# Cross attention: outputs turned in 32x32 blocks, operations dealt out over the steps, second round in front of the first, hand-over in source order

## The chip, the cores and the metric

The kernel runs on one core of a Trainium2 chip. The metric is the time of one execution on the device in microseconds (us), taken as the median of several runs. Engines are named as the profile names them: PE (TensorE, matrix multiply) and PEld (its weight loads), DVE (VectorE), ACT (ScalarE), POOL (GpSimd), SP (SyncE, which here only issues DMAs).

## The reference

One pre-norm decoder layer on x of 32 x 128 x 512 in float32: self attention, cross attention, then a mixture of experts with a shared expert.

```python
x = x + _L0_attn_ref(_layernorm(x, axis=-1), ...)             # differential attention, 16 heads, causal
x = x + _L0_xattn_ref(_layernorm(x, axis=-1), ctx_2048, ...)   # this change
x = x + _L0_ffn_ref(_layernorm(x, axis=-1), ...)               # 32 experts, 6 per token, and a shared expert

# cross attention: 128 channels of 512 positions; 8 heads of 16 channels; for each of 32 batches
q, k, v = split_heads(Wq x + bq), split_heads(Wk c + bk), split_heads(Wv c + bv)
q, k = rotary(q), rotary(k)
p = softmax(q k^T / 4)                      # 512 x 512 for each head
out = Wo (p v) + bo

# experts: scores = sigmoid(x @ gate_w); of 4 groups of 8 experts the two with the best maxima are masked out,
# the best 6 of the rest are taken, weights divided by their sum;
# expert(x) = (silu(x @ w_gate) * (x @ w_up)) @ w_down; the shared expert has the same form for all tokens
```

## The kernel before, in words

**Stages.** Self attention runs to about 870 us and writes x1 to DRAM. The cross attention (class `CrossAttention`) follows to about 2058 us. Behind it lie two groups of the shared expert (class `Shared`, 4 batches of 128 tokens a group), among which the rest of the routing is put (the hand-over). From about 2212 us the routed experts run (class `Experts`, 208 tiles of 128 token slots), from about 3748 us the other six groups of the shared expert.

**A step of the cross attention.** Work is cut into 512 steps (b, side, c, pair): 32 batches, two sides (even and odd heads), four chunks of 128 positions, two pairs of heads. In a first round `maxima` (two matmuls of 32 rows by 512 columns, L621) computes scores and DVE takes row maxima from PSUM (L625). When the 8 steps of a side are done, `turn_maxima` transposes the maxima and adds them to the queries (L633). Eleven steps later the second round, `exponentials`, computes the same scores the other way round, already shifted (L644), and ACT takes exp (L648). `weigh` multiplies values and exponentials (L659), in two halves before and behind the two rounds of a step, once for each 8 steps. A column of ones beside the values gives the denominators. The two rounds of one step use different row quarters of the array.

**The other operations of a batch.** `plan` gives each a step number: `sooner` ones come in front of the two rounds of a step, `later` ones behind them. In order: `load`, `project` and `rotate` for keys and queries (DVE shuffle L590, five POOL operations), `measure` and `normalize`; after weighing, ACT copies the weighed outputs out of PSUM (`xu`, L665), `divide` turns them with 8 TensorE transposes (L674), takes reciprocals (L677) and multiplies (L680), `turn_out` turns them back with 4 transposes (L83) and an ACT copy, `leave` applies Wo (L697) and adds (L701). Then `measure_out`, `normalize_out`, `hand_over` (h3 and its transpose to DRAM), `router`, and the routing: `groups`, `choose`, `take` (L928, L933), `count` (two matmuls L940, L941), `slots_of`, six times `enter` (one indirect DMA from POOL, L957). A batch's routing ends some 60 steps after its attention, so the operations of four batches lie among the steps of a fifth.

**What sets the order.** `CrossAttention.run` holds PE, DVE, ACT and POOL to source order (`manual_schedule`). An instruction that waits holds all behind it on its engine. Everything else, the hand-over among it, is ordered by a scheduler of the framework. PSUM is used through 4 buffers of two banks each (`Common.banks`); an operation that takes one waits until the last reader of its former content is done.

**Hand-over before.** Group 0 of the shared expert runs with `between` called 8 times; each of six calls runs 16 steps' worth of the remaining operations (`cross.rest(16)`), then come `routing.tiles` (which expert has which tiles) and a DMA. Then `Experts.__init__` gathers the tables from DRAM (L1215), turns them (L1224, L1234) and works out addresses (L1239 to L1257); `begin` starts tokens and weights; group 1 runs; then the expert loop.

Of the kernel before, what the change touches and what calls it, by code (L numbers as in the profile page):

```python
# [10 lines left out]
F32 = mybir.dt.float32  # L11
# [7 lines left out]
P = 128  # L19
# [444 lines left out]
class CrossAttention:  # L464
# [12 lines left out]

    NH, C = 8, 16
# [172 lines left out]
    def weigh(self, b, side, half):  # L651
# [11 lines left out]
        if half:  # L663
            self.out[b, side] = self.p2.tile([P, E], F32, name="xu")
            self.nc.scalar.copy(self.out[b, side], po.pop((b, side)))  # L665

    def divide(self, b):

        nc, TC, Q, C, out = self.nc, self.TC, self.Q, self.C, self.out
        tr = self.cm.banks()  # L670
        for side in range(2):
            u = out.pop((b, side))
            for c in range(TC):
                nc.tensor.transpose(tr[:, side, ts(c, P)], u[:, ts(c, P)], self.cm.ident)  # L674
        tr = tr.rearrange("p s (x r) -> p s x r", r=2 * C)
        rs = self.p2.tile([P, 2, TC * Q], F32, name="xrs")
        nc.vector.reciprocal(rs, tr[:, :, :, C])  # L677
        out[b] = self.p2.tile([P, TC * Q, 2, C], F32, name="xo")
        for side in range(2):
            nc.vector.tensor_tensor(  # L680
                out[b][:, :, side, :], tr[:, side, :, 0:C],
                rs[:, side].unsqueeze(2).broadcast_to([P, TC * Q, C]), ALU.mult,
            )

    def turn_out(self, b):
        tr = self.cm.turn4(self.out.pop(b).rearrange("p x s c -> p (x s c)"))
        self.out[b] = self.p2.tile([P, self.TC, P], F32, name="xoT")
        self.nc.scalar.copy(self.out[b], tr)
# [5 lines left out]
    def leave(self, b):  # L694
# [3 lines left out]
            py, self.wT["o"], self.out.pop(b).rearrange("p t x -> p (t x)"), start=True, stop=True  # L698
# [30 lines left out]
    def plan(self, load_shared):  # L729

        S, later, sooner, routing = self.S, self.later, self.sooner, self.routing
        for b in range(self.B):
# [16 lines left out]
            sooner.put(at + 29, self.measure_out, b)  # L749
            later.put(at + 31, self.normalize_out, b)  # L750
            later.put(at + 38, self.hand_over, b)
            later.put(at + 40, self.router, b)
            later.put(at + 45, routing.groups, b)
            sooner.put(at + 53, routing.choose, b)
            later.put(at + 53, routing.take, b)
            later.put(at + 55, routing.count, b)
            sooner.put(at + 61, routing.slots_of, b)
            for k in range(TOPK):
                later.put(at + 63 + 5 * k // 2, routing.enter, b, k)
        later.put(20, load_shared)  # L760
        for b in range(self.B):
            sooner.put(2 * S * b - 11, self.measure, b)
# [12 lines left out]
    def advance(self, count, end=None):  # L775
# [3 lines left out]
        for _ in range(count):  # L779
# [6 lines left out]
            self.sooner.run(n)  # L786
            if 0 <= n < len(steps):
                self.maxima(*steps[n])
            if 0 <= n - behind < len(steps):
                self.exponentials(*steps[n - behind])  # L790
# [27 lines left out]
class Routing:  # L818
# [61 lines left out]
    def groups(self, b):  # L880

        nc = self.nc
        s = self.score.pop(b)
# [5 lines left out]
        )  # L889
        top = self.small("g_top", [P, 8])  # L890
# [202 lines left out]
class Shared:  # L1093
# [6 lines left out]
    def __init__(self, cm, pool, w, h3T_d, sum_d, out):  # L1100
        self.cm, self.pool, self.w, self.h3T_d, self.sum_d, self.out = cm, pool, w, h3T_d, sum_d, out
        self.NB = h3T_d.shape[0]
        self.hTs = {}

    def load(self, g):
        G = self.G
        if g * G < self.NB and g not in self.hTs:
            self.hTs[g] = self.pool.tile([P, G, EC, P], F32, name="s_hT", bufs=2)
            self.cm.nc.sync.dma_start(
                out=self.hTs[g], in_=self.h3T_d[ts(g, G)].rearrange("b p c t -> p b c t")  # L1110
            )

    def group(self, g, final, between=lambda: None):
# [4 lines left out]
        self.load(g)  # L1118
        self.load(g + 1)
        hT = self.hTs.pop(g)  # L1120
        gu = pool.tile([P, n + 1, G, P], F32, name="s_gu")
        for m in range(n):
            pgu = cm.banks().rearrange("p two (i t) -> p two i t", i=G)
            for i, part in enumerate((w.gate, w.up)):
                for c in range(EC):
# [3 lines left out]
                    )  # L1129
            act = pool.tile([P, G, P], F32, name="s_act", bufs=2)  # L1130
# [43 lines left out]
class Experts:  # L1174
# [210 lines left out]
    def begin(self, first, end):  # L1385

        self.first, self.end, self.last = first, end, None
        for i in range(first, first + 3):
            self.tokens(i)
# [187 lines left out]
```

## Time and profile before

| what | value |
|---|---|
| median of 3 runs | 4100.53 us (4096.46 to 4104.73) |
| profiled execution | 4099.66 us, span of its instructions 4098.0 us |
| mean granted TensorE clock | 0.992 |
| DMA | 386 MB moved by the core's queues, mean 94 GB/s |
| cross-attention loop, per batch | 37.13 us |
| hand-over, last weighing to first expert matmul | 153.7 us |
| one group of the shared expert | 57.5 us |

The page of a profile gives the busy time of each engine, the busy share in 40 slices of the span (a digit is tenths), the chain of work that ended last, and groups of equal instructions. A group's row reads: line, engine, operation, output <- inputs, shapes, count, busy us and mean ns of one. Views of the trace give a timeline (start, duration, engine, line, operation; in brackets the idle time in front and what ended it), waits (who waited for whom), windows (busy us of each engine in a stretch) and single lines (minimum, median and maximum in ns). A matmul of 512 columns in float32 has two records. Records of one engine overlap a little, so the distance from start to start is shorter than a duration.

### The profile page before, as it was taken

What the parts mean: (1) busy time and instruction counts of PE and PEld (TensorE: products, weight loads), DVE (VectorE), ACT (ScalarE), POOL (GpSimd) and SP (SyncE); (2) the same over time, 40 slices, a digit from 0 to 9 for tenths busy, and PEclk for the clock granted to TensorE, in tenths of its full rate; (3) what the DMA queues carried; (4) which work ended last, traced back from release to release, by engine and by line L of the source; (5) the groups of instructions that cost most, each with busy time, mean ns of one, the idle gap of its engine ahead of it and who ended that gap; (6) DMA issues with size and microseconds to landing.
All of it is one profiled execution on the core that took longest, in us unless ns stands there. A gap on an engine that the chain in (4) does not pass through costs nothing. (4 is left out here: it accounts for less than half of the span.)

```text
span 4098.0 us, 59001 instructions
## 1 busy us (share of the span) xinstructions
PE 3979.2 (97%) x20404; PEld 2081.9 (51%) x20404; DVE 2192.4 (54%) x3461; ACT 1245.6 (30%) x1791; POOL 2241.5 (55%) x2420
## 2 busy tenths in 40 slices
PE   7999999989999999999979999999999999999999
PEld 5666666533344444434335555555555555554444
DVE  5777777777888888888722333333333333332111
ACT  3333333235555555555510111111111111111000
POOL 3444444443555555555444777777777777772000
PEclk9999999999999999999999999999999999999999
DMA  3111110021111111111134777686777776774110
GB/s 105 32 32 31 32 32 27 32 80 38 46 45 40 45 45 45 42 42 45 32 125 117 173 171 195 139 198 155 175 158 174 167 182 155 179 179 115 52 62 31
DMA packets 282785, 386.24 MB, mean 94 GB/s; under 512 B 147792, under 2 KB 175056, under 8 KB 282448
## 3 DMA queue, kind: packets, MB, share of 16 engines
q0 software_dynamic: 62912, 109.85, 15.0%
q1 hardware_dynamic: 77680, 186.52, 14.0%
q10 hardware_dynamic: 141888, 86.01, 7.6%
q8 instruction: 165, 2.70, 0.3%
q14 instruction: 140, 1.15, 0.1%
HBM read 616.47 MB, written 142.02 MB: 185 GB/s over the span
## 5 line engine op out<-in xcount | busy, mean ns | idle before, releaser
L1310 POOL DMA_INDIRECT e_xr<-h_d,e_run_of x832 | 849.4, 1021 | 296.3 <-issue 246.8
L625 DVE TENSOR_REDUCE nm<-ps 128x2 f32<-128x1024 f32 x512 | 623.2, 1224 | 199.6 <-PE ps L621 131.4
L648 ACT ACTIVATE xp<-ps 128x1024 f32<-128x1024 f32 x512 | 516.8, 1023 | 432.0 <-PE ps L644 430.3
L1340 DVE TENSOR_TENSOR e_gu<-e_act,ps 128x352 f32<-128x352 f32 x208 | 108.4, 521 | 956.4 <-ACT e_act L1339 956.4
L1371 PE MATMUL ps<-wd,e_guT 128*128 128x512 f32 (+1 forms) x1248 | 571.7, 594 | 2.2 <-issue 2.1
L621 PE MATMUL ps<-xk,xq 32*128 32x512 f32 x2048 | 564.3, 635 | 6.7 <-DVE xres L403 4.3
L644 PE MATMUL ps<-xqn,xk 32*128 32x512 f32 x2048 | 548.1, 638 | 0.6 <-DVE xqn L633 0.6
L1335 PE MATMUL ps<-wg,e_xT 128*128 128x352 f32 x1664 | 527.7, 459 | 4.2 <-DMA wg<-in_L_ffn_w_gate_dram 3.4
L1335 PE MATMUL ps<-wu,e_xT 128*128 128x352 f32 x1664 | 527.1, 460 | 2.0 <-DMA wu<-in_L_ffn_w_up_dram 1.9
L1335 PEld LDWEIGHTS ps<-wg,e_xT 128*128 128x128 f32 x1664 | 314.8, 189 | 238.3 <-issue 103.4
L1335 PEld LDWEIGHTS ps<-wu,e_xT 128*128 128x128 f32 x1664 | 316.4, 190 | 179.7 <-DMA wu<-in_L_ffn_w_up_dram 3.7
L1376 POOL DMA_INDIRECT sum_d<-e_y,e_into x208 | 338.3, 1627 | 116.7 <-issue 65.0
L1339 ACT ACTIVATE e_act<-ps 128x352 f32<-128x352 f32 x208 | 96.3, 463 | 892.8 <-PE ps L1335 818.4
L1371 PEld LDWEIGHTS ps<-wd,e_guT 128*128 128x128 f32 (+1 forms) x1248 | 238.0, 191 | 247.5 <-issue 204.1
L1375 ACT ACTIVATE e_y<-ps,e_weight 128x512 f32<-128x512 f32 x208 | 142.9, 687 | 421.6 <-PE ps L1371 407.2
L621 PEld LDWEIGHTS ps<-xk,xq 32*128 32x128 f32 x2048 | 158.6, 183 | 220.6 <-ACT xp L648 100.4
L957 POOL DMA_INDIRECT table_d<-entry,at x192 | 196.6, 1024 | 108.7 <-DMA table_d<-entry,at 55.0
L1361 DVE STREAM_TRANSPOSE e_guT<-e_gr 96x384 f32<-96x384 f32 (+1 forms) x416 | 230.3, 554 | 37.9 <-DMA e_gr<-e_gu_d 30.6
L659 PE MATMUL ps<-xp,v 128*32 128x512 f32 x2048 | 247.1, 598 | 3.0 <-ACT xp L648 2.6
L1322 DVE STREAM_TRANSPOSE e_xT<-e_xr 128x512 f32<-128x512 f32 x208 | 226.7, 1090 | 6.4 <-DMA e_xr<-h_d,e_run_of 6.4
L239 POOL TENSOR_SCALAR k<-kz,a_keep,a_extra 128x256 f32<-128x256 f32 x128 | 69.8, 555 | 252.4 <-ACT kz L238 252.4
L644 PEld LDWEIGHTS ps<-xqn,xk 32*128 32x128 f32 x2048 | 152.8, 183 | 37.6 <-DVE nm L625 25.6
(265 smaller groups left out, 5071.9 us busy)
## 6 DMA issues: line engine op xcount, KB each, us to landing
wg<-in_L_ffn_w_gate_dram SPq DMA_DIRECT2D x208, 704.0 KB
wu<-in_L_ffn_w_up_dram SPq DMA_DIRECT2D x208, 704.0 KB
wd<-in_L_ffn_w_down_dram SPq DMA_DIRECT2D x208, 576.0 KB
e_gu_d<-e_gu ACTq DMA_DIRECT2D x208, 192.0 KB
e_gr<-e_gu_d ACTq DMA_DIRECT2D x208, 192.0 KB
wd<-in_L_ffn_w_down_dram SPq DMA_DIRECT2D x208, 128.0 KB
e_xr<-h_d,e_run_of POOLq DMA_INDIRECT x832
xin<-in_x_dram SPq DMA_DIRECT2D x32, 256.0 KB
```

What stands on the lines that cost most here:

```text
L621: self.nc.tensor.matmul(sc[:, i, :], q[rows, ts(c, P)], k[rows, :], start=True, stop=True)
L625: self.nc.vector.tensor_reduce(at[:, self.ROW[side], 2 * pair : 2 * pair + 2], sc, AX.X, ALU.max, negate=True)
L644: self.nc.tensor.matmul(sc[:, i, :], k[rows, ts(c, P)], q[rows, :], start=True, stop=True)
L648: self.nc.scalar.activation(e, sc, AF.Exp)
L659: self.nc.tensor.matmul(po[b, side][ts(j, 32), :], self.v2[b % 2][:, c, 2 * j + side, :], es[j // 2][:, j % 2, :], start=c == 0, stop=c == ...
L957: self.nc.gpsimd.indirect_dma_start(out=self.table_ds[k % 2][:, :], out_offset=bass.IndirectOffsetOnAxis(ap=self.at[b][:, k : k + 1], axis=0),
L1310: self.cm.nc.gpsimd.indirect_dma_start(out=xr[:, t, :], out_offset=None, in_=self.h3_d.rearrange("t (q f) -> (t q) f", q=self.Q), in_offse ...
L1322: self.cm.nc.vector.transpose(xT.rearrange("p c (t i) -> p c t i", t=self.Q), self.xr.pop(i).rearrange("p t (j c) -> p c t j", c=EC),)
L1335: nc.tensor.matmul(pgu[:, half, 0:M], t[:, c, :], w[:, c, :], start=c == 0, stop=c == EC - 1)
L1361: self.cm.nc.vector.transpose(t[rows, 0:n, :].rearrange("p c (t i) -> p c t i", t=self.Q), g[rows, :, 0 : 32 * n].rearrange("p t (j c) -> ...
L1371: nc.tensor.matmul(py, t[:n, c, :], self.wd[s][:n, c, :], start=c == 0, stop=c == len(M_CHUNKS) - 1)
L1376: nc.gpsimd.indirect_dma_start(out=self.sum_d[:, :], out_offset=bass.IndirectOffsetOnAxis(ap=self.into[:, i : i + 1], axis=0), in_=y[:, :] ...
```

## The change

Five things are done.

1. *Outputs turned in blocks.* DVE transposes the weighed outputs of a side out of PSUM in blocks of 32 x 32 (two instructions a batch, in `weigh`) into one tile `xu` of both sides. `divide` takes reciprocals and multiplies in one instruction for both sides; `turn_out` is one more DVE block transpose. The 12 TensorE transposes and 3 ACT copies of a batch are gone, and with them two PSUM buffers.
2. *Step numbers.* `measure`, `measure_out`, `normalize_out` come 1 or 2 steps earlier, `groups` is cut in two (`sigmoid` first), the routing operations come 1 or 2 steps later.
3. *Order in a step.* `exponentials` stands in front of `maxima`.
4. *Hand-over.* It is held to source order on PE, DVE, ACT and POOL. Two groups of the shared expert carry 33 calls of `cross.rest(2)`, with `between` also called in the middle of each chunk and in the down projection. A third group, which stood at the end, is moved in front of the experts and carries the tables' work, which is cut in `fetch`, `arrange`, `turn_tables`, `places`, `first_tokens`.
5. *Loads.* The first tokens of the shared expert (`load_tokens`) and the rows that a group adds to (`load_rows`) are loaded earlier; the tiles `s_hT` have a pool of their own.

```diff
         if half:
-            self.out[b, side] = self.p2.tile([P, E], F32, name="xu")
-            self.nc.scalar.copy(self.out[b, side], po.pop((b, side)))
+            if side == 0:
+                self.out[b] = self.p2.tile([P, 2, E // 32, 32], F32, name="xu", bufs=1)
+            self.nc.vector.transpose(
+                self.out[b][:, side].rearrange("p k r -> p (k r)"), po.pop((b, side))
+            )
     def divide(self, b):
-        nc, TC, Q, C, out = self.nc, self.TC, self.Q, self.C, self.out
-        tr = self.cm.banks()
-        for side in range(2):
-            u = out.pop((b, side))
-            for c in range(TC):
-                nc.tensor.transpose(tr[:, side, ts(c, P)], u[:, ts(c, P)], self.cm.ident)
-        tr = tr.rearrange("p s (x r) -> p s x r", r=2 * C)
-        rs = self.p2.tile([P, 2, TC * Q], F32, name="xrs")
-        nc.vector.reciprocal(rs, tr[:, :, :, C])
-        out[b] = self.p2.tile([P, TC * Q, 2, C], F32, name="xo")
-        for side in range(2):
-            nc.vector.tensor_tensor(
-                out[b][:, :, side, :], tr[:, side, :, 0:C],
-                rs[:, side].unsqueeze(2).broadcast_to([P, TC * Q, C]), ALU.mult,
-            )
+        nc, C = self.nc, self.C
+        u, n = self.out.pop(b), E // 32
+        rs = self.p2.tile([P, 2, n], F32, name="xrs")
+        nc.vector.reciprocal(rs, u[:, :, :, C])
+        self.out[b] = self.p2.tile([P, n, 2, C], F32, name="xo")
+        nc.vector.tensor_tensor(
+            self.out[b].rearrange("p k s c -> p s k c"), u[:, :, :, 0:C],
+            rs.unsqueeze(3).broadcast_to([P, 2, n, C]), ALU.mult,
+        )
     def turn_out(self, b):
-        tr = self.cm.turn4(self.out.pop(b).rearrange("p x s c -> p (x s c)"))
-        self.out[b] = self.p2.tile([P, self.TC, P], F32, name="xoT")
-        self.nc.scalar.copy(self.out[b], tr)
+        o = self.out.pop(b)
+        self.out[b] = self.p2.tile([P, E], F32, name="xoT")
+        self.nc.vector.transpose(self.out[b], o.rearrange("p k s c -> p (k s c)"))
...
-            sooner.put(at + 29, self.measure_out, b)
-            later.put(at + 31, self.normalize_out, b)
+            sooner.put(at + 27, self.measure_out, b)
+            later.put(at + 29, self.normalize_out, b)
             later.put(at + 38, self.hand_over, b)
             later.put(at + 40, self.router, b)
-            later.put(at + 45, routing.groups, b)
-            sooner.put(at + 53, routing.choose, b)
-            later.put(at + 53, routing.take, b)
-            later.put(at + 55, routing.count, b)
-            sooner.put(at + 61, routing.slots_of, b)
+            later.put(at + 43, routing.sigmoid, b)
+            later.put(at + 46, routing.groups, b)
+            sooner.put(at + 55, routing.choose, b)
+            later.put(at + 55, routing.take, b)
+            later.put(at + 56, routing.count, b)
+            sooner.put(at + 63, routing.slots_of, b)
             for k in range(TOPK):
-                later.put(at + 63 + 5 * k // 2, routing.enter, b, k)
+                later.put(at + 65 + 5 * k // 2, routing.enter, b, k)
         later.put(20, load_shared)
+        later.put(2 * S * (self.B - 2), load_tokens)
         for b in range(self.B):
-            sooner.put(2 * S * b - 11, self.measure, b)
+            sooner.put(2 * S * b - 12, self.measure, b)
...
             self.sooner.run(n)
+            if 0 <= n - behind < len(steps):
+                self.exponentials(*steps[n - behind])
             if 0 <= n < len(steps):
                 self.maxima(*steps[n])
-            if 0 <= n - behind < len(steps):
-                self.exponentials(*steps[n - behind])
...
+    def load_rows(self, g):
+        if g not in self.x2s:
+            self.x2s[g] = []
+            for pair in range(self.G // 2):
+                x2 = self.pool.tile([P, 2, E], F32, name="s_x2", bufs=2)
+                self.cm.nc.sync.dma_start(out=x2, in_=self.rows_of(g, pair))
+                self.x2s[g].append(x2)
...
+    def fetch(self):
+        nc = self.cm.nc
+        for j in range(self.NT):
+            self.got[j] = [
+                self.p2.tile([P, E], F32, name=("e_y", "e_xT")[j % 2])[:, 0 : 2 * P].rearrange(
+                    "p (s o) -> p s o", o=2
+                )
+                for i in range(len(self.table_ds))
+            ]
+            for t, table_d in zip(self.got[j], self.table_ds):
+                nc.gpsimd.indirect_dma_start(
+                    out=t.rearrange("p s o -> p (s o)"),
+                    out_offset=None,
+                    in_=table_d.rearrange("(n s) o -> n (s o)", s=P),
+                    in_offset=bass.IndirectOffsetOnAxis(ap=self.rows[:, j : j + 1], axis=0),
+                    bounds_check=table_d.shape[0] // P - 1,
+                )
+        nc.gpsimd.memset(self.gu_s, 0.0)
+        nc.gpsimd.iota(self.row_i, pattern=[[0, 2]], base=self.T + 1, channel_multiplier=1)
+    def arrange(self, j):
+        nc = self.cm.nc
+        got = self.got[j]
+        nc.vector.tensor_tensor(got[0], got[0], got[1], ALU.add)
+        runs = self.spread[j] = self.p2.tile([P, self.Q, self.Q, 32], F32, name="e_xr", bufs=3)
+        slots = got[0][:, :, 0].rearrange("p (b t a) -> p t a b", b=self.Q, t=self.Q)
+        for t in range(self.Q):
+            nc.vector.tensor_copy(
+                runs[:, t].rearrange("p q (a b) -> p q a b", b=self.Q),
+                slots[:, t].unsqueeze(1).broadcast_to([P, self.Q, 32 // self.Q, self.Q]),
+            )
+    def turn_tables(self):
+        nc, cm = self.cm.nc, self.cm
+        self.entry_ps = cm.banks().rearrange("p o (j t) -> p o j t", j=EC)
+        self.parts_ps = cm.banks().rearrange("p o (t j x) -> p (o t) j x", t=2, j=2)
+        for j in range(self.NT):
+            got, runs = self.got.pop(j), self.spread.pop(j)
+            for o in range(2):
+                nc.tensor.transpose(self.entry_ps[:, o, j, :], got[0][:, :, o], cm.ident)
+            for t in range(self.Q):
+                nc.tensor.transpose(
+                    self.parts_ps[:, t, j, :], runs[:, t].rearrange("p q i -> p (q i)"), cm.ident
+                )
+    def places(self):
+        nc, cp, T, n_tiles = self.cm.nc, self.cp, self.T, self.n_tiles
+        entry = self.entry_ps.rearrange("p o j t -> p o (j t)")[:, :, 0:n_tiles]
+        self.weight = cp.tile([P, n_tiles], F32, name="e_weight")
+        nc.vector.tensor_copy(self.weight, entry[:, 1, :])
+        row_i, row = self.row_i, self.row
+        nc.vector.tensor_scalar(row_i[:, 1:2], row_i[:, 1:2], -T - 1, None, ALU.add)
+        nc.vector.tensor_scalar(row_i[:, 1:2], row_i[:, 1:2], 5, None, ALU.logical_shift_right)
+        nc.vector.tensor_copy(row, row_i)
+        self.run_of = cp.tile([P, self.Q, self.NT * P], I32, name="e_run_of")
+        nc.vector.tensor_scalar(
+            self.run_of, self.parts_ps.rearrange("p t j x -> p t (j x)"), float(self.Q),
+            float(-self.Q), ALU.mult, ALU.add,
+        )
+        nc.vector.tensor_scalar(self.run_of, self.run_of, 0.0, row[:, 1:2], ALU.max, ALU.add)
+        none = cp.tile([P, n_tiles], F32, name="e_none")
+        nc.vector.tensor_scalar(none, entry[:, 0, :], 0.0, row[:, 0:1], ALU.is_equal, ALU.mult)
+        self.into = cp.tile([P, n_tiles], I32, name="e_into")
+        nc.vector.scalar_tensor_tensor(self.into, entry[:, 0, :], -1.0, none, ALU.add, ALU.add)
+    def first_tokens(self):
+        for i in range(self.first, self.first + 3):
+            self.tokens(i)
...
-        todo = [lambda: cross.rest(16)] * 6 + [
+        shared.use(s_pool, s_w)
+        en = mybir.EngineType
+        in_order = {en.PE, en.DVE, en.Activation, en.Pool}
+        todo = [lambda: cross.rest(2)] * 33 + [
             lambda: routing.tiles(eid, fresh, rows, used, usual),
             lambda: nc.sync.dma_start(out=sum_d[T : T + P, :], in_=rest),
         ]
-        EARLY = 2
-        shared.group(0, False, between)
+        EARLY = 3
+        with tc.manual_schedule(engines=in_order):
+            for g in range(EARLY - 1):
+                shared.group(g, False, between)
+            while todo:
+                between()
+    e_ctx = ctx.enter_context(ExitStack())
+    with tc.manual_schedule(engines=in_order):
+        experts = Experts(
+            cm, e_ctx, table_ds, h3_d, sum_d, w_gate, w_up, w_down, eid, fresh, rows, n_tiles
+        )
+        shared.load_rows(EARLY - 1)
+        experts.begin(0, usual)
+        experts.fetch()
+        nothing = lambda: None
+        todo += [nothing] * 3 + [
+            lambda: experts.arrange(0),
+            lambda: experts.arrange(1),
+            nothing,
+            experts.turn_tables,
+            experts.places,
+            experts.first_tokens,
+        ]
+        shared.group(EARLY - 1, False, between)
         while todo:
             between()
-    experts = Experts(
-        cm, e_ctx, table_ds, h3_d, sum_d, w_gate, w_up, w_down, eid, fresh, rows, n_tiles
-    )
-    experts.begin(0, usual)
-    for g in range(1, EARLY):
-        shared.group(g, False)
     experts.run()
```

## The prediction

> **What bounds the kernel now.** I read the page first: which engine is busy, then in which slices it isn't.
>
> ```profile
> span 4098.0 us, 59001 instructions
> PE 3979.2 (97%) x20404; PEld 2081.9 (51%) x20404; DVE 2192.4 (54%) x3461; ACT 1245.6 (30%) x1791; POOL 2241.5 (55%) x2420
> PE   7999999989999999999979999999999999999999
> ```
>
> TensorE is busy for 97% of the span, so time is saved by taking work off it or by closing its gaps. The change touches two stretches: the cross-attention loop (about 905 to 2058 us) and the hand-over behind it (slice 21 of 40). The table of windows gives one batch of the loop, then the hand-over from the last weighing matmul to the first expert matmul, then one undisturbed group of the shared expert.
>
> ```profile
> 1414.79:1451.92 37.13, 36.51 (x243) 15.02 (x242) 30.01 (x51) 21.87 (x27) 21.05 (x30) 1.00 0.14 44
> 2058.20:2211.94 153.74, 131.41 (x352) 62.28 (x351) 34.36 (x103) 17.40 (x26) 54.88 (x74) 0.93 0.40 127
> 3747.96:3805.50 57.54, 57.54 (x145) 26.35 (x145) 5.49 (x8) 3.74 (x7) 1.55 (x1) 1.00 0.31 97
> ```
>
> Columns: length, busy us of PE, PEld, DVE, ACT, POOL, granted clock, DMA share, GB/s. A batch takes 37.13 us with DVE busy for 30.0. But a busy PE also counts a matmul that runs alone where two could run side by side. That is read from the timeline of TensorE:
>
> ```profile
> 1421.22 1.13 PE L621 MATMUL ps<-xk,xq 32*128 32x512 f32 x4
> 1422.02 1.13 PE L644 MATMUL ps<-xqn,xk 32*128 32x512 f32 x4
> 1423.08 0.41 PE L940 MATMUL ps<-taken,before 128*128 128x32 f32 x2
> 1440.87 1.09 PE L674 MATMUL ps<-ident,xu 128*128 128x128 f32 x8
> 1443.29 0.63 PE L83 MATMUL ps<-ident,xo 128*128 128x128 f32 x4 [0.20 <-DVE xo L680]
> 1450.87 1.12 PE L580 MATMUL ps<-cx,kT 128*128 128x512 f32 x2 [0.41 <-DVE nm L625]
> ```
>
> The first-round (L621) and second-round (L644) matmuls of a step start together and take 1.07 us from start to next start. Here L644 comes 0.80 late and the step takes 1.86. Summing start distances: 16 steps x 1.07 = 17.1; weighing 4 x 1.85 = 7.4; three projections 1.05 each; values 1.09; two turns of maxima and h3, 0.59 each; count 0.56; router 1.01; the transposes of xu 1.02 and xo 0.55. That is 33.7. The other 3.45 of the 37.13 are late partners and waits.
>
> The hand-over's waits, from the timeline:
>
> ```profile
> 2062.50 5.53 PE L1126 MATMUL ps<-s_hT,sg 128*128 128x512 f32 x8 [4.23 <-DMA s_hT<-h3T_d]
> 2088.47 0.41 PE L940 MATMUL ps<-taken,before 128*128 128x32 f32 x2 [2.80 <-DVE taken L933]
> 2101.99 0.38 PE L940 MATMUL ps<-taken,before 128*128 128x32 f32 x2 [3.34 <-DVE taken L933]
> 2130.54 7.38 PE L1158 MATMUL ps<-sd,s_gu 128*128 128x512 f32 x12 [7.25 <-DVE s_gu L1132]
> 2154.66 0.54 PE L1224 MATMUL ps<-ident,e_y 128*128 128x128 f32 x2 [2.40 <-DVE e_y L1222]
> ```
>
> With three smaller ones (1.33, 0.68, 0.31) they add to 22.3. Two groups at 57.5 and 9.5 of small matmuls need 124.5 of the 153.7, so 29.2 is lost; the 7 beyond the waits are matmuls at a lower clock (0.93 here; the 5.53 above against 3.60 later).
>
> **The change, part by part: the loop.** TensorE loses 12 transposes per batch: 1.02 + 0.55, so its work is 32.1. ACT loses three copies (two of 0.585, one of 0.580). DVE gains two transposes of a 128x512 out of PSUM: no row has it; by L339 (128x768, 974 ns) scaled, 0.67; by L386 (698, from SBUF), 0.70; I take 0.67, about 0.60 from start to next start. It gains one transpose out of SBUF (L386: 0.70, interval 0.65). The two products of 0.42 become one of 128x512 with both inputs in SBUF.
>
> ```profile
> L352 DVE TENSOR_TENSOR o<-u,rs x64: 668/693/1528, 75.4 to 859.9; 128x512 f32<-128x512 f32 x64
> L928 DVE TENSOR_TENSOR hits<-number,picked x32: 346/1334/1368, 1010.4 to 2101.0; 128x192 f32<-128x192 f32 x32
> ```
>
> [...] If it always met a 1.28 us product of the rotation, the row's maximum (1.53) applies, 0.83 more. L928 shows the same spread: 1.33 in the loop, where it starts behind a rotation product on POOL, 0.35 in the hand-over. In the new order `take` comes two steps later, after POOL's rotation of the keys, and POOL's rotation of the queries ends some 3 us before the product. So I take 0.69 for the product and 0.35 for `hits`, and keep the other ends. DVE is then about 30.5 per batch: no bound by itself.
>
> Then the order. In the program as built, the PSUM buffer of a step's maxima is mostly that of the exponentials one step before, and buffers of exponentials wait for reductions. Times from the rows: an ACT exp starts 1.28 after its matmuls, lasts 1.02, and frees the buffer 0.05 later (2.35 in all); a reduction starts 1.17 after its matmuls, the next DVE work 1.14 later, the buffer is free 1.28 after its start (1420.74 to 1422.02 for the late L644 above). I follow one batch from the first weighing half at step 5 (modulo 16), t = 0. Weighing, step, weighing: step 6 at 4.77. Step 7's maxima wait for step 6's exp: 7.12, 0.69 lost. Its reduction at 8.29, `take` from 9.43 (0.40 + 0.54): `count`, which TensorE reaches at 9.26, starts at 10.37, 1.11 lost. Queued behind it on TensorE are the router and all of step 9, and DVE waits for both. Count and router 1.57: step 9 at 11.94, step 10's maxima at 14.29 (0.69 lost), its reduction at 15.46, the moved measure_out 1.08, step 11's reduction at 17.68, the next weighing at 18.96 (0.41 lost). 4.77 later step 14, step 15's maxima at 26.08 (0.19 lost), reduction at 27.25. From there DVE doesn't pause: reduction 1.14, divide 1.05, 1.14, turn_out 0.65, 1.14, turned maxima 0.62, 1.14, then leave's sum frees a buffer 0.80 later: step 4's maxima at 34.93 (1.86 lost on the way), with the projection the next batch starts at 37.05. Losses 4.97 + work 32.1 = 37.05. So the 1.57 saved is given back, mostly to the wait of `count` and the DVE run behind `divide`: 37.05 against 37.13. Bounds: losses as now, 33.7 + 3.45 - 1.57 - 0.2 = 35.4; [...] 37.05 + 0.98 + 0.83 = 38.9. Over 31 batches: -2.5 (from -54 to +55). The drain after the last maxima has the transposes and two waits too: -1.5.
>
> Edits with no cost here: the sixfold `enter` (1.0 us each on POOL), now also ahead of the query rotation; that rotation still ends about 2 us before its first use, and if it didn't, step 0 would be that much later. `sigmoid` split off: same instructions. `load_tokens`: 1 MB on SP's queue during a loop that uses DMA to 14%.
>
> **The hand-over.** Source order, 2 steps between half-chunks of 3.43 us each. s_hT lies ready: no 4.23. `take` and `count` are 1 call apart, and each call leaves DVE under 3 us of work, so 2.80 and 3.34 go. The table's tail (`tiles`) runs on DVE at the end of group 1: about 31 instructions of 0.2 plus the last sum, rows ready at 8 us into group 2; four gathers (1.07 each) and a landing of up to 5.1 (the DVE wait on e_y): arranged by 19; turn_tables comes at 24: no 2.40. Its runs are placed by 33, the first tokens' gather (9.5 from there to the first turned tile in the trace) by 43, the second by 46. In the built order both turned tiles stand on DVE ahead of the last s_gu pieces, which TensorE needs at 48.5: 2 us of cover; later tokens stall TensorE one for one. Weights are issued on SP as soon as eid is there (group 2 + 10) and needed at 57. The third group is moved: 57.5 less at the end, 57.5 more here. Its copy to the output grows from 2.1 to 3.1 MB, in SP's queue before the rows of the next group; that traffic now ends by 3769 and the first rows are used at 3796, so 27 us cover it. Three groups 172.4 + 9.5 - 1.57 = 180.3, against 153.7 + 57.5 = 211.2: at most 30.9. For waits the order brings I leave 3: -28 (bounds -31 and -10, if half of the old waits return).
>
> **Sum** against the span: 4098.0 - 2.5 - 1.5 - 28 = 4066.0. The profiled execution took 4099.66 and the median of the runs is 4100.53, 2.5 above the span: 4068.5 predicted.
>
> **Rivals.** (1) TensorE's saving stays: a batch takes 35.4, 4068.5 - 51 = 4017. For it: 7.1 us of DVE idle per batch. Against: the chain above has no slack. 0.17. (2) [...] 38.9, +57: 4126, slower. Price 1.81 per batch; from 38.4 on (1.3 above my 37.05) the kernel is slower than before by over 0.2%. `hits` alone, 38.0, gives 4098: no change. For it: 1.33 in 27 of 27 loop batches. Against: POOL's place at that time. 0.11. (3) The hand-over keeps half its waits (DVE in source order holds s_gu behind tokens or tables): 4083 to 4092. 0.17. My forecast: 0.55, by itself 4050 to 4084.
>
> **How the numbers follow.** Under 4030 lie about two thirds of (1), over 4095 the slower part of (2), together 0.19: 4030 to 4095. A measurement of this kernel tells 0.2% (8.2 us) from no change. Faster: 0.55 + 0.17 + 0.13 of (3) = 0.85; within 0.2%: 0.04 of (3) and 0.03 of (2) = 0.07; slower: 0.08.
>
> **What would show it.** One batch from first weighing to first weighing near 37.0; TensorE waiting about 1.1 per batch for `taken` before `count`; `hits` at 0.35 in the loop and the product at 0.7; the first expert matmul 180 to 184 us behind the last weighing, granted clock 1.00 there. A batch under 36.3 or over 37.8 makes the forecast wrong by its loop term; more than 190 us in the hand-over, by the other.

## The result and the profile after

The kernel after takes 4078.16 us (median of 5 runs, 4077.86 to 4082.92), the kernel before 4101.96 beside it (5 runs): a ratio of 0.9941 (95% interval 0.9925 to 0.9957), 24 us less. The forecast was 4068.5. The profiled execution of after is the slowest of its five (4082.92, span 4081.2). First the page of after:

```profile
span 4081.2 us, 58193 instructions
...
PE 3925.0 (96%) x20020; PEld 2048.3 (50%) x20020; DVE 2198.9 (54%) x3525; ACT 1196.3 (29%) x1695; POOL 2247.3 (55%) x2420
...
PE   7999999989999999999999999999999999999999
```

TensorE has 384 instructions less and the digit 7 of slice 21 (the hand-over) has become a 9. The table of windows of after, for one batch of the loop and for the hand-over (length, busy us of PE, PEld, DVE, ACT, POOL, granted clock, DMA share, GB/s):

```profile
1401.36:1439.03 37.67, 34.75 (x231) 13.76 (x231) 29.95 (x52) 20.32 (x25) 21.33 (x30) 0.95 0.15 45
...
2067.85:2251.84 183.99, 181.46 (x486) 85.36 (x482) 45.20 (x137) 19.97 (x31) 59.63 (x85) 0.99 0.37 113
```

The hand-over is what was forecast: three groups in 184.0 us at a clock of 0.99. The loop is not. A batch is 0.5 longer than before, and the clock stands at 0.95 where it was 1.00. The same batch, cut in four:

```profile
1401.36:1428.30 26.94, 25.78 (x180) 9.44 (x180) 21.98 (x38) 14.60 (x17) 19.21 (x27) 1.00 0.19 60
1428.30:1431.10 2.80, 1.46 (x15) 1.42 (x13) 2.60 (x6) 1.02 (x1) 0.96 (x2) 1.00 0.02 4
1431.10:1434.90 3.80, 3.80 (x19) 1.75 (x22) 2.01 (x3) 1.96 (x3) 0.32 (x1) 0.55 0.00 0
1434.90:1439.03 4.13, 3.72 (x27) 1.15 (x19) 3.35 (x6) 2.74 (x4) 0.83 (x2) 1.00 0.09 13
```

The whole loss of clock lies in 3.8 us (third line, 0.55), right behind a stretch in which TensorE has little to do (second line: busy for 1.46 of 2.80 us). The timeline of TensorE shows what that stretch is:

```profile
1427.73 0.59 PE L646 MATMUL ps<-xqn,xk 32*128 32x512 f32 x2
1429.67 0.38 PE L945 MATMUL ps<-taken,before 128*128 128x32 f32 x2 [1.34 <-DVE taken L938]
...
1430.11 1.06 PE L724 MATMUL ps<-gw,h3T 128*128 128x32 f32 x8
1431.10 0.88 PE L646 MATMUL ps<-xqn,xk 32*128 32x512 f32 x2
...
1431.76 1.07 PE L646 MATMUL ps<-xqn,xk 32*128 32x512 f32 x2
...
1432.79 1.11 PE L83 MATMUL ps<-ident,nm 128*128 128x128 f32 x4
1433.83 1.21 PE L646 MATMUL ps<-xqn,xk 32*128 32x512 f32 x2
```

`count` waits 1.34 us for `taken`, and `count` and the router behind it are matmuls of 32 columns. Then the L646 pairs take 0.88, 1.07 and 1.21 where they take 0.70 and 0.59 elsewhere, and the turn at L83 takes 1.11 where it takes 0.66. The table of TensorE's waits between 1000 and 2000 us (who waited for whom: us in total, times, longest) has this wait first, in each of 27 batches; the kernel before has no wait for `taken` there:

```profile
PE ps L945 <- DVE taken L938: 36.3, 27, 1.4
PE ps L697 <- DVE nm L627: 15.7, 27, 0.6
PE ps L646 <- DVE nm L627: 10.6, 26, 0.5
```

By terms, from the two profiled executions (us; start, loop and drain are cut at the first and last projection of the queries and at the end of the last weighing):

| term | forecast | measured |
|---|---|---|
| start | 0 | +0.1 |
| loop | -2.5 | +14.5 |
| drain of the loop | -1.5 | -5.0 |
| hand-over with the group moved out of the end | -28 | -26.5 (+30.2 in front of the experts, -56.7 behind) |
| span | -32.0 | -16.8 |

So the question for the experiments is the loop. The theory T: the wait of `count` and the low clock behind it are its whole loss. Rivals: the clock falls for another reason (R1); the run of DVE sets the batch and the wait only moves (R2).

### The profile page after: what moved, and what is told of

Its sections match the earlier page's. It is cut to its first block, busy times and chain, and to the rows that moved or that the text cites. A ratio compares the mean times of both kernels' runs of the same rounds, so it can differ in the third digit from the quotient of the medians.

```text
span 4081.2 us, 58193 instructions
## 1 busy us (share of the span) xinstructions
PE 3925.0 (96%) x20020; PEld 2048.3 (50%) x20020; DVE 2198.9 (54%) x3525; ACT 1196.3 (29%) x1695; POOL 2247.3 (55%) x2420
## 5 line engine op out<-in xcount | busy, mean ns | idle before, releaser
L627 DVE TENSOR_REDUCE nm<-ps 128x2 f32<-128x1024 f32 x512 | 623.5, 1220 | 184.1 <-PE ps L623 184.0
L646 PE MATMUL ps<-xqn,xk 32*128 32x512 f32 x2048 | 585.2, 660 | 20.0 <-DVE nm L627 12.2
L646 PEld LDWEIGHTS ps<-xqn,xk 32*128 32x128 f32 x2048 | 173.2, 195 | 270.4 <-ACT xp L650 68.8
L623 PEld LDWEIGHTS ps<-xk,xq 32*128 32x128 f32 x2048 | 166.8, 195 | 43.7 <-ACT xp L650 13.7
```

Source lines behind the costliest of these rows:

```text
L623: self.nc.tensor.matmul(sc[:, i, :], q[rows, ts(c, P)], k[rows, :], start=True, stop=True)
L627: self.nc.vector.tensor_reduce(at[:, self.ROW[side], 2 * pair : 2 * pair + 2], sc, AX.X, ALU.max, negate=True)
L646: self.nc.tensor.matmul(sc[:, i, :], k[rows, ts(c, P)], q[rows, :], start=True, stop=True)
```

## The experiments

A "batch" below is the distance from one projection of the queries to that of the next batch, mean of 21 batches: 37.14 before, 37.64 after. Ratios are to the kernel before, run in the same series.

**`count` one step later.** Kernel after with

```diff
-            later.put(at + 56, routing.count, b)
+            later.put(at + 57, routing.count, b)
```

> Kernel after, with `count` one step later (57 instead of 56), so that its wait for `taken` falls in the shadow of one more step. Theory T (the wait of 1.34 us before `count` and the low clock in the 4 us behind it, 1.6 us by the distances of its matmuls, are the whole loss of the loop): a batch takes 34.7 to 35.7 instead of 37.67, the granted clock in the loop is 1.00 again, total 3985 to 4015. Rival R1 (the clock of 0.95 has another cause): only the wait goes, a batch takes about 36.3, clock 0.95, total about 4037. Rival R2 (DVE's run sets the length of a batch, the wait only moves): 37.3 or more, total within 12 us of 4078.

Measured: ratio 0.9822 (0.9800 to 0.9844), a batch 35.99. A window and the first of its waits:

```profile
1343.45:1379.42 35.97, 33.40 (x231) 13.14 (x231) 29.77 (x52) 20.17 (x25) 21.36 (x30) 1.00 0.14 45
```

```profile
PE ps L646 <- ACT xp L650: 29.0, 56, 0.9
```

The clock is 1.00 again, so R1 falls. One number brings 1.65 per batch, but not the 2.9 that wait and clock make together: T is too simple. In place of the wait for `taken` TensorE now waits 1.0 per batch for exponentials, so part of the wait moved, as R2 has it.

**The router in front of `count`.** Kernel after with

```diff
-            later.put(at + 40, self.router, b)
+            later.put(at + 39.5, self.router, b)
```

> Kernel after, with the router's matmuls (1.01 us) in front of `count` in the same step, so that the wait for `taken` ends when it did, but TensorE idles only 0.3 us before it. T: 1.0 us of the wait is filled and the clock stays at 1.00, which is worth 1.6 more: a batch takes about 35.1, total about 3997. R1 (the clock isn't due to this wait): 36.7, clock 0.95, total about 4047. R2: 37.3 or more, total within 12 us of 4078.

Measured: ratio 0.9878 (0.9860 to 0.9896), a batch 36.56 in the mean. It is not one length but two kinds: 35.8 to 36.2 in some batches, 37.0 to 38.6 in others. The router, now in front of the waiting `count`, starts at 1161.26 and `count` at 1162.68; in the kernel after it starts only behind it (1430.11 and 1429.67). Two batches in the timeline, the wait the same in both:

```profile
1162.68 0.38 PE L945 MATMUL ps<-taken,before 128*128 128x32 f32 x2 [0.34 <-DVE taken L938]
...
1164.78 0.66 PE L83 MATMUL ps<-ident,nm 128*128 128x128 f32 x4
...
1198.60 0.38 PE L945 MATMUL ps<-taken,before 128*128 128x32 f32 x2 [0.34 <-DVE taken L938]
...
1201.64 1.11 PE L83 MATMUL ps<-ident,nm 128*128 128x128 f32 x4
```

With 0.34 of idle time and the same 1.4 us of 32-column matmuls the clock falls in one batch and holds in the next. In the windows of these two places it is 1.00 (1162.0 to 1166.4) and 0.67 (1198.0 to 1202.8). It is the clock, not the wait, that makes the two kinds.

The trace of the kernel after holds the same comparison. Its wait is 1.34 in all 28 batches, but behind 4 of them the clock held. Batches without a drop of the clock take 36.3 to 37.0, with a drop of 3.41 us 37.5 to 37.9, with one of 6.83 us 39.1 to 39.3. One drop, and two batches without any (counted from `count` to `count`), as windows:

```profile
1431.49:1434.90 3.41, 3.41 (x18) 1.44 (x14) 1.82 (x2) 1.90 (x3) 0.00 (x0) 0.50 0.00 0
1845.01:1881.65 36.64, 33.83 (x230) 13.32 (x231) 29.93 (x52) 20.32 (x24) 21.32 (x30) 1.00 0.13 44
1881.65:1918.29 36.64, 33.83 (x230) 13.32 (x231) 29.93 (x52) 20.33 (x24) 21.32 (x30) 1.00 0.15 44
```

What tells the two kinds apart is the place in time. In the trace of after, the 24 drops of the loop start 37.55 us apart (20 times), 40.96 (once) or 112.63 (twice): 11, 12 and 33 times 3.413. Call a time that lies a whole multiple of 3.413 us from the start of a drop a mark. In the kernel after the clock falls where `count` starts 0.8 to 2.7 us behind a mark (24 batches) and holds at the other places seen, 3.0 to 4.0 (4 batches; 3.4 to 4.0 is up to 0.6 behind the next). With the router in front, where the marks are an estimate from the first slow matmul behind `count` (1.22 us from 1199.64 on), it falls at 1.1 to 2.4 us (10 batches) and holds at the others (18). The 37.55 from drop to drop is close to a batch of 37.64, so the place hardly moves from one batch to the next and drop follows drop. That part of the loss is an accident of the length.

**The wait filled with useless matmuls.** Kernel after; the results of the added matmuls are used by nothing, and all else is computed as before:

```diff
-        pp = self.cm.banks()[:, 0, 0 : 2 * NX]
+        pp = self.cm.banks()
+        for i in range(8):
+            nc.tensor.matmul(
+                pp[:, 1, ts(i % 4, P)], self.cm.ident, self.cm.ident, start=True, stop=True
+            )
+        pp = pp[:, 0, 0 : 2 * NX]
```

> Kernel after with eight useless matmuls (128x128, about 1.2 us, written to an unused part of the same PSUM buffer) in front of `count`'s two, so that TensorE works while it waits for `taken`; `count` still can't start before `taken` is there. New theory C, from the two runs before (without the wait a batch took 35.98 at full clock, with a wait of 0.34 it took 35.8 to 35.9 where the clock stayed and 37.1 to 38.6 where it fell): the wait itself is taken up by slack behind it, and the loss is the low clock that follows a stretch in which TensorE does little (2.8 us here: wait, `count`, router). So more work must make it faster: a batch of 35.8 to 36.2, clock 1.00, about 50 us less than the kernel after (ratio to before about 0.982). Rival W (the wait costs its length, clock aside): 37.5 or more, no gain.

Measured: ratio 0.9910 (0.9892 to 0.9928), a batch 37.05 at a clock of 1.00. More work made the kernel faster, but by 0.6 per batch only: neither 36 nor 37.5. The eight took 1.89 us (1343.18 to 1345.07) and not 1.2, and `count` came 0.5 late:

```profile
1343.18 2.05 PE L946 MATMUL ps<-ident 128*128 128x128 f32 x16
1345.07 0.31 PE L950 MATMUL ps<-taken,before 128*128 128x32 f32 x2
```

So with five (`range(5)`):

> Kernel after with five useless matmuls in the wait of `count` instead of eight (eight took 1.9 us and ran 0.5 us past the arrival of `taken`; five take 1.2). `count` starts when it does in the kernel after, 0.1 to 0.2 us behind the filler. Theory C: clock 1.00, a batch shorter than the 37.05 of eight by the 0.5 or so of overrun, 36.4 to 36.7; the distance to 37.64 is what the low clock costs, the distance to 35.98 what the late start of `count` costs. If the clock is still below 0.98, the filler is too short and the batch stays over 37.

Measured: ratio 0.9871 (0.9854 to 0.9887), a batch 36.60, clock 1.00. Its timeline:

```profile
1339.11 1.38 PE L946 MATMUL ps<-ident 128*128 128x128 f32 x10
1340.44 0.41 PE L950 MATMUL ps<-taken,before 128*128 128x32 f32 x2
...
1340.91 1.06 PE L724 MATMUL ps<-gw,h3T 128*128 128x32 f32 x8
1341.90 0.70 PE L646 MATMUL ps<-xqn,xk 32*128 32x512 f32 x2
...
1342.97 0.66 PE L83 MATMUL ps<-ident,nm 128*128 128x128 f32 x4
```

From the second weighing half (1333.03) to the first matmul of the step behind the router it is 8.87 us here; in the kernel after it is 8.92 (1422.18 to 1431.10). Up to there the two are alike, and then only the clock differs. That splits the 1.65: the low clock costs 37.64 - 36.60 = 1.04 per batch, the late start of `count` costs 36.60 - 35.99 = 0.61. The batches of the kernel after in which the clock held, 36.64 above, say the same without any filler. Theory C, that the wait itself costs nothing, was wrong by these 0.61.

**The wait brought into the kernel before.** First by one step:

```diff
-            later.put(at + 55, routing.count, b)
+            later.put(at + 54, routing.count, b)
```

> The kernel before with one number changed: `count` at step 54 instead of 55, one step behind `take`, as it stands in the kernel after. T: a wait of 1 to 2 us for `taken` appears in each batch and the granted clock of the loop falls from 1.00 to about 0.95; a batch takes 39.5 to 41, total 4175 to 4220. R1 (a wait of this length leaves the clock at 1.00): 38.2 to 39, total 4130 to 4155. R2 (slack elsewhere takes the wait up): within 12 us of 4101.

Measured: ratio 0.9987 (0.9980 to 0.9995), a batch 36.88. A miss: the wait is 0.26 only, the clock stays at 1.00, and the batch is shorter by 0.26 (why, no run shows). Step 53 has a weighing half behind it, which stands between `take` and `count`:

```profile
1302.98 1.92 PE L659 MATMUL ps<-xp,v 128*32 128x512 f32 x16
1306.24 0.38 PE L940 MATMUL ps<-taken,before 128*128 128x32 f32 x2 [0.26 <-DVE taken L933]
```

So TensorE reaches `count` only 4.07 us behind the start of the step of `take`; in the kernel after it is 2.64, with no weighing between. DVE is done with `taken` 4.2 and 3.8 us behind that start: it is TensorE's side that differs. The run says nothing of a longer wait. Then with `take` and `count` both in step 56, in front of the router:

```diff
-            later.put(at + 53, routing.take, b)
-            later.put(at + 55, routing.count, b)
+            later.put(at + 56, routing.take, b)
+            later.put(at + 56, routing.count, b)
```

> The kernel before with `take` and `count` both in step 56, in front of the router of step 40 of the next batch: a wait of 1.3 us or more for `taken`, with `count` and the router right behind it, as in the kernel after. C: the granted clock falls to about 0.95 in the loop and each batch takes 1.6 us or more longer than 37.14 (38.7 to 40), total 50 to 90 above before. If the clock in the kernel after falls for another reason (less work on TensorE in the loop, or the new order), the clock stays at 1.00 here and a batch takes 37.0 to 38.5.

Measured: ratio 1.0209 (1.0192 to 1.0226), a batch 40.48. Waits and a window of it:

```profile
PE ps L940 <- DVE taken L933: 54.8, 25, 2.2
```

```profile
1300.00:1620.00 320.00, 295.80 (x1914) 126.26 (x1916) 230.66 (x390) 171.85 (x214) 165.38 (x236) 0.95 0.13 40
```

The old loop, at a clock of 1.00 without this wait, falls to 0.95 with it. The batch is 3.34 longer for a wait of 2.19 (here too the clock held behind 4 of 28 waits). So the clock goes with the wait, not with the block transposes or the new order.

**The hand-over alone.** Kernel before with parts 4 and 5 of the change. Against the kernel after, the loop's parts are put back, in short:

```diff
-            self.nc.vector.transpose(
-                self.out[b][:, side].rearrange("p k r -> p (k r)"), po.pop((b, side))
-            )
+            self.nc.scalar.copy(self.out[b, side], po.pop((b, side)))
...
-            later.put(at + 56, routing.count, b)
+            later.put(at + 55, routing.count, b)
...
-            if 0 <= n - behind < len(steps):
-                self.exponentials(*steps[n - behind])
             if 0 <= n < len(steps):
                 self.maxima(*steps[n])
+            if 0 <= n - behind < len(steps):
+                self.exponentials(*steps[n - behind])
```

> The kernel before with the hand-over of the kernel after alone (parts 4 and 5 of the change; loop, outputs and step numbers as before). T: 27 us less than before, total 4072 to 4077, so below the kernel after: the loop's parts cost about 9. Rival: the hand-over's gain needs the new loop's drain; total 4085 or more.

Measured: ratio 0.9918 (0.9897 to 0.9940); a batch 37.14; from last weighing to first expert matmul 181.1. The interval holds the expected 27 us (0.9934). The hand-over doesn't need the new loop. Against the 0.9941 of the kernel after, the loop's parts as built cost about 9 us, as expected; but the two intervals overlap, so this difference is not clear of noise.

**The parts of the loop, one by one.** Three kernels, all with the new hand-over. The block transposes alone on the old loop (the first piece of the diff above left as it is in the kernel after, with `divide`, `turn_out` and `leave`):

> Old step numbers and old order of the rounds, new hand-over, and of the loop's changes only the block transposes on DVE (12 transposes of TensorE fewer in a batch, two on DVE more). If TensorE's work sets the batch, 37.14 - 1.57 = 35.6; if the run of DVE behind `divide` takes part of it back, as the prediction has it, 36.2 to 37.0. Clock 1.00, since `count` has two steps behind `take`. Against the old loop with the new hand-over (0.9918 of before): 5 to 48 us less.

The order of the rounds alone on the old loop (the last piece left as it is in the kernel after):

> Old loop with new hand-over, and of the loop's changes only the order in a step: exponentials in front of maxima. Outputs turned by TensorE as before, old step numbers. If the order of the rounds is good by itself, a batch takes 36.0 to 36.8 instead of 37.14; if it pays only together with the block transposes (where it took the batch from 37.53 to 35.98), 37.0 to 38. Clock 1.00: `count` has two steps behind `take`.

And the new loop with `count` at 57, but the old order:

```diff
-            if 0 <= n - behind < len(steps):
-                self.exponentials(*steps[n - behind])
             if 0 <= n < len(steps):
                 self.maxima(*steps[n])
+            if 0 <= n - behind < len(steps):
+                self.exponentials(*steps[n - behind])
```

> The new kernel with `count` at step 57 (a batch of 35.98) and the old order of the two rounds in a step, first round in front. If the waits of the maxima for PSUM buffers that exponentials hold are what the new order brings (about 0.9 and 0.3 per batch), they go and a batch takes 35.0 to 35.7; if the order of the rounds hides DVE's run, a batch takes 36.3 or more. Clock 1.00 either way.

Measured, as us of one batch, all at a clock of 1.00:

| | first round in front | second round in front |
|---|---|---|
| turned by TensorE, old step numbers | 37.14 | 36.55 |
| turned in blocks, old step numbers | 37.06 | not run |
| turned in blocks, new numbers, `count` at 57 | 37.53 | 35.99 |

Ratios: block transposes alone 0.9935 (0.9919 to 0.9952), order alone 0.9887 (0.9868 to 0.9906), third kernel 0.9950 (0.9933 to 0.9966). Twelve transposes less on TensorE are worth 0.08 in the old order, and with the new step numbers a batch is 0.47 longer there (37.06 to 37.53). Where the saving went is seen in the timeline of the block transposes alone, behind `divide`:

```profile
1439.45 1.13 PE L623 MATMUL ps<-xk,xq 32*128 32x512 f32 x4
1440.79 1.36 PE L646 MATMUL ps<-xqn,xk 32*128 32x512 f32 x8 [0.21 <-DVE nm L627]
1441.75 1.29 PE L623 MATMUL ps<-xk,xq 32*128 32x512 f32 x8
1443.10 1.13 PE L646 MATMUL ps<-xqn,xk 32*128 32x512 f32 x4
```

The two rounds, which should start together, run one behind the other: a step takes two lengths of 1.1. DVE works from 1437.4 to 1447.5 without a wait, so it is what paces this stretch (read from the trace). TensorE's saving turns into late partners that a profile counts as busy: with 1.57 less work in a batch, its busy time falls only from 36.52 to 36.30. The new order is worth 0.59 by itself and 1.54 together with the blocks and the new numbers.

**DVE's run broken up, and the turned tiles put behind s_gu.** Kernel after with `count` at 57 and

```diff
-            later.put(at + 16, self.turn_out, b)
-            later.put(at + 18, self.leave, b)
+            later.put(at + 18, self.turn_out, b)
+            later.put(at + 20, self.leave, b)
...
             experts.first_tokens,
+            nothing,
+            nothing,
+            lambda: experts.turn_in(0),
+            lambda: experts.turn_in(1),
         ]
```

(in `Experts.run` the two tiles are then not turned again).

> Kernel after with `count` at 57 and two more edits. Loop: `turn_out` at step 18 instead of 16 and `leave` at 20 instead of 18, so that DVE's run behind `divide` is broken up; if that run is what delays TensorE there (waits of 0.17, 0.41 and 0.59 and 0.3 of late maxima in a batch), a batch falls from 35.98 to 35.0 to 35.7; if the waits only move, 35.9 to 36.3. Hand-over: the first two turned token tiles stand behind the last pieces of s_gu on DVE, called in the down projection; the wait of 2.51 and the low clock behind it (20 matmuls in 10.55 instead of 8.85) go, the first expert matmul comes 180 to 181 us behind the last weighing instead of 184. Total 30 to 45 less than the kernel with `count` at 57 was below before, so a ratio to before of 0.970 to 0.980.

Measured: 4018.67 us, ratio 0.9792 (0.9775 to 0.9808), the lowest ratio of all. A batch takes 35.71: that is 0.28 less. The wait in front of `leave` (0.6) is gone, but one for the turned maxima (15.9 us in 28 batches, 0.57 each) has come, so the batch is at the upper edge of what was expected if DVE's run is the delay (35.0 to 35.7). The hand-over takes 178.5; with `count` at 57 alone it was 185.1. Its last matmuls, without wait and at full clock:

```profile
2165.87 8.75 PE L1181 MATMUL ps<-sd,s_gu 128*128 128x512 f32 x20
2174.55 1.13 PE L1188 MATMUL ps<-sd,s_gu 64*128 64x512 f32 x4
2175.61 8.85 PE L1181 MATMUL ps<-sd,s_gu 128*128 128x512 f32 x20
```

## Why the prediction was right, and where not

**Sign and size.** 4068.5 was forecast for the likeliest case (by itself 4050 to 4084), 4078.16 came. The hand-over brought the gain; the loop was to give 2.5 and took 14.5. So the loop's term had the wrong sign and was off by 17.0; that the total stayed in the range of 4030 to 4095 is luck as far as the loop goes, since the range was that wide for a saving that stays (rival 1) and for long times of `hits` and of the new product (rival 2), not for the clock, and the drain gave 3.5 more than forecast. In the sums small things are off: the named losses of the loop add to 4.95 (4.97), three groups of 57.54 to 172.6 (172.4), and half of the 29.2 lost is 14.6, which gives the 4083 of rival 3 but neither its 4092 nor the bound of -10.

**Hand-over (-28 forecast, -26.5 measured).** Right in its steps. The waits for s_hT, for `taken` and for the table's rows are gone. The first expert matmul comes 184.0 behind the last weighing (forecast 180 to 184). Of the 3 us left for new waits, one wait was named as covered by 2 us: the last s_gu pieces behind the turned tiles on DVE. This cover failed. Counted from the start of the third group (2187.91), the gather of the first tokens was issued at 34.0 (33 forecast), but its tile was turned at 45.8 (43) and the second at 48.9 (46): from issue to turn it took 11.8 us, not 9.5. TensorE's timeline:

```profile
2238.39 1.98 PE L1188 MATMUL ps<-sd,s_gu 64*128 64x512 f32 x4 [2.51 <-DVE s_gu L1173]
2240.30 10.55 PE L1181 MATMUL ps<-sd,s_gu 128*128 128x512 f32 x20
```

the issue on POOL and DVE's timeline:

```profile
2221.95 1.06 POOL L1356 DMA_INDIRECT e_xr<-h_d,e_run_of  x1 [20.70 <-issue]
2233.75 1.10 DVE L1368 STREAM_TRANSPOSE e_xT<-e_xr 128x512 f32<-128x512 f32 x1 [8.54 <-DMA e_xr<-h_d,e_run_of]
2236.80 1.08 DVE L1368 STREAM_TRANSPOSE e_xT<-e_xr 128x512 f32<-128x512 f32 x1 [1.96 <-DMA e_xr<-h_d,e_run_of]
2237.91 0.42 DVE L1173 TENSOR_TENSOR s_gu<-s_act,ps 64x256 f32<-64x256 f32 x1
```

The second tile's tokens landed only at 2236.8, and the pieces stood behind it. Why the landing took longer than forecast stays open. The 20 matmuls that follow take 10.55 instead of 8.85, the low clock again (granted 0.50 from 2240.45 to 2243.86). The last experiment undoes it: 2.5 of wait and 1.7 of clock are gone, and the hand-over takes 178.5, 5.4 less (6.6 less than with `count` at 57 alone; the edit of `leave`, which acts in the drain too, is in the same number).

**Loop (37.05 forecast, 37.64 measured).** The path was right step by step. The maxima of step 7 start 0.65 behind their partner (forecast 0.69). `count` waits 1.34 (1.11). Step 9 starts 11.85 behind the first weighing half (11.94). That TensorE's 1.57 is given back to a run of DVE behind `divide` is what the block transposes alone show: 37.06. The side of a batch that holds this run takes 17.89 (18.09). What failed is the price of the wait of `count`: it was counted by its length, with TensorE at full clock on the other side. The other side of the batch was to take 18.96. It takes 18.69 with the wait filled, and 19.78 as the kernel stands: 1.09 of low clock that no term of the sum held, and 0.27 + 0.20 of waits put too high, which hide a part of it. The trace of before had the sign of it: the prediction itself put 7 us of the old hand-over, with waits of 2.4 to 7.3, down to matmuls at a lower clock, and did not carry this over to a wait of its own.

**The costs on DVE (rival 2).** In rival 2 `hits` and the new product take the long times of the rows L928 and L352, 1.33 and 1.53, in every batch, which makes it 38.9 long (the author's estimate). That did not come. Single lines of after, minimum, median and maximum in ns:

```profile
L933 DVE TENSOR_TENSOR hits<-number,picked x32: 348/350/359, 1013.3 to 2152.9; 128x192 f32<-128x192 f32 x32
L680 DVE TENSOR_TENSOR xo<-xu,xrs x32: 691/692/736, 927.2 to 2069.2; 128x512 f32<-128x512 f32 x32
L668 DVE STREAM_TRANSPOSE xu<-ps x64: 716/717/718, 907.0 to 2068.0; 128x512 f32<-128x512 f32 x64
```

`hits` takes 0.35 in every batch (1.33 before), the product 0.69 (before, two of 0.42), both the values taken. The transpose out of PSUM takes 0.72 (0.67). POOL's place is what the prediction had against rival 2, and it differs as forecast: when `hits` starts, POOL is at an `enter` in the kernel after (started 0.72 earlier, in 27 of 28 batches), where it was at a rotation product in the kernel before (started 0.15 earlier, 1.27 long, in 27 of 27). That POOL's instruction is the cause of the long `hits` is the author's estimate; no run moved it alone.

**Rival 1 (35.4, the saving stays).** Not in this kernel, but the prediction's argument against it, that the chain has no slack, was too strong: with `count` one step later a batch takes 35.99. Rival 3 (half of the old waits stay) is out by the 184.0.

**Drain (-1.5 forecast, -5.0 measured).** Put too low; no experiment was made on it.

## What to carry to other kernels

A wait on a busy TensorE can cost more than its length (1.34 of wait cost 1.65 a batch, 2.19 cost 3.34), or nothing (0.26). Look at the granted clock behind it: here 3.41 us at 0.50 stood behind most waits of 1.34 (24 of 28), and five matmuls of 128x128 put into the wait kept it at 1.00. Since one trace holds waits of 1.34 with a drop (24) and without (4), compare single batches of a trace before building a kernel to find its price. Work taken off the busiest engine is only gained where the second engine's run isn't what paces it (here 1.57 a batch taken off brought 0.08), and whether two partner matmuls start together shows this better than the busy share. The distance of two operations on different engines is to be counted in work between them, not in steps: one step with a weighing half between was nearly enough (wait 0.26), one without was not (1.34).

## What the runs showed of the hardware

- In this loop the granted clock falls from 1.00 to 0.50 for 3.41 us, sometimes 6.83, and in the trace of after all 24 drops start whole multiples of 3.413 us apart (37.55, 40.96, 112.63). In the kernel after, 2.80 us in which TensorE was idle for 1.34 and else ran 32-column matmuls brought a drop in 24 of 28 batches. With 0.34 of idle time and the same matmuls it was 10 of 28; with the idle time filled, none (clock 1.00 from 1000 to 2000 us). How little work brings a drop, no run here measures.
- Eight float32 matmuls of 128x128 took 1.89 us, 0.24 each, with two records each; eight transposes of the same size take 1.02 (the turn of xu in the kernel before), with one record each. That is why the first filler ran over.
